# Attention by single key blocks from the third block of an image on, and outputs at fixed places of a block

## The chip, the cores and the metric

The kernel runs on one core of a Trainium2 chip. The metric is the device time of one execution in microseconds. The times shown are of three runs, of which the median counts; a profile was taken of one further execution.

## What is computed

The input x is four images of 128 channels and 64 x 64 points, all in 32-bit floats. Cut to what matters here:

```python
x = x + conv_part(group_norm(x))          # layer 0: convolution, norms, and a selective scan (Mamba)
t = tokens(x)                             # 4 images x 4096 tokens x 128
qkv = layer_norm(t) @ W_qkv + b_qkv       # 4 heads of 32
scores = einsum('bhnd,bhmd->bhnm', q, k) / sqrt(128)
t = t + (softmax(scores) @ v) @ W_proj + b_proj
t = t + experts(layer_norm(t))            # 8 experts, the two best of each token, weighted
```

The scan of layer 0 runs along the 4096 points of an image: h = da * h + du for 16 states of each channel. The attention is over all 4096 tokens of the same image. So an image's attention needs keys and values of all its points, while queries and keys of a point exist as soon as layer 0 is done there.

## The kernel before

**Units of work.** An image is cut into 8 blocks of 512 points. The kernel's main loop (L1207 to L1254, the `while slot < len(units) ...` loop) runs *slots*. Each of the slots 0 to 1023 holds one unit of the scan: image b, block i, channel half p, state n, in this order, so that a block takes 32 slots. A unit is one exponential on ScalarE (da), a multiply, the scan itself and a second multiply on VectorE (tiles h and hc), and a matmul with the identity that sums over the states (y), for single states in the first 128 slots and later for sums of two states, which GpSimd makes.

**Attention groups.** Beside its scan unit a slot holds one attention group, if the generator `attention` has one to give. A group is two key tiles of 128 keys against 1024 queries of one head: four score matmuls (sc), two exponentials of 128 x 1024 (pT), and, one slot later in `weighted`, eight matmuls with the values (av). Each image has 4 query sets (q) x 4 heads x 32 key tiles, so 256 groups, and all four have 1024. The exponential needs no maximum, since the scores' size is bounded ahead, so partial sums over some of the keys may be stored and added later. Groups come in the order of RUNS: one entry is a query set and the key quarters (two blocks each) that it is taken over. In a run each head has its parts (one key quarter, four groups). A run that does not end a query set's keys stores its sum (avs, by way of ScalarE, to the DRAM tile avd); the next run of the same query set loads it as prev and adds it on GpSimd. When the last run of a set is done, the sum goes to the DRAM tile total, `inverted` makes the reciprocals of the softmax's denominators (inverse), and two outputs are put on lane X.

**When a group can run.** `quarters_ready` asks whether the blocks of the part's queries and keys are closed, that is, whether their queries, keys and values are on their way to DRAM. If not, the slot goes on without a group. Groups are taken strictly in order; an image's groups begin when the image before has had its 256. The loads of the next part (ks, v, and qs for a new head) are issued with the second of a part's four groups, on SP's queue, where all loads and stores of the main loop are issued in order. There are 3 buffers of ks and v and 2 of qs, prev and avs, and one PSUM buffer of av.

**Lanes.** Everything else is in two lanes of small steps, X and Y, that advance two steps in each slot (`advance`). Lane Y makes what the scan needs (first_norm, conv, inputs), in a fixed order. Lane X holds `closed` of each block (what comes after the scan, down to keys, queries and values), which is put at its front when the block's scan is done, and the outputs (`finished`: projection, norm, routing, experts, store), which stand at its back. A task of a lane runs to its end before the next begins, so that an output under way delays the next closed. After slot 1023 lane Y takes outputs from lane X as well, if it has nothing else.

**Order.** The wrapper at L445 chains each engine's instructions in the order in which the Python program issues them, so nothing is reordered, and the profile gives L445 for almost every instruction: tiles' names tell them apart. The order, and so the number of slots, is fixed when the program is built. In the program of before there are 1204 slots; the first group is in slot 78, the last in slot 1177.

Of the kernel before, what the change touches and what calls it, by code (L numbers as in the profile page):

```python
# [9 lines left out]
F32 = mybir.dt.float32  # L10
F32R = mybir.dt.float32r
# [6 lines left out]
P = 128  # L18
C = 128
EPS = 1e-5  # L20
BLK = 512
NT = BLK // P
IMG = 64
DI = 64
NST = 16
DH = 32
NH = 4
# [9 lines left out]
def conv_mamba_attn_moe_kernel(ctx: ExitStack, tc: tile.TileContext, t: dict):  # L37
    nc = tc.nc
    x, out = t["x"], t["out"]
    B, _, L = x.shape  # L40
    NB = L // BLK
# [727 lines left out]
    def closed(b, i):  # L769

        if i == 0:
            kqv[b] = [], [], [], dram.tile([P, NTILE * C], F32, name="td")
        kd, qd, vd, td = kqv[b]
        j, u = divmod(i, 2)
        if u == 0:
            kd.append(dram.tile([P, 2, 2 * BLK], F32, name=f"kd{j}"))
            qd.append(dram.tile([P, 2, 2, 2 * BLK], F32, name=f"qd{j}"))
            vd.append(dram.tile([NH, 2, P, NT * 2 * DH], F32, name=f"vd{j}"))
        kd, qd, vd, sj = kd[j], qd[j], vd[j], slice(u * BLK, (u + 1) * BLK)
        s = slice(i * BLK, (i + 1) * BLK)  # L780
        cm = tmp("X", "cm")
        vector.scalar_tensor_tensor(
            cm.rearrange(IMAGE, w=IMG), xn_of[b, i][:, 3:].rearrange(IMAGE, w=IMG), skip,
            y0_rows(b, i), ALU.mult, ALU.add,
        )
        xr = load_x(t["xtok"][b], i, "xr")
        yield
        yield
        ps = work("X")
        for p in range(2):  # L790
            r = slice(DI * p, DI * p + DI)
            mm(ps[r, :], wout[:, p, r], gated.pop((b, i, p)))
        done.add(("freed", b, i))
        yield
        vector.tensor_add(cm, ps, cm)
        gpsimd.tensor_add(by_tile(xr), by_tile(xr), projb[:, None, :].to_broadcast([P, NT, C]))
        yield
        while held:
            yield
            yield  # L800
        held.add("closed")
        ps = transposed("X", by_tile(cm))
        yield
        xt = yield from normalised("X", by_tile(ps))
        held.clear()
        ps = transposed("X", xt)
        yield
        f = tmp("X", "f")
        scalar.activation(f, ps, AF.Identity, bias=lnb, scale=lnw)
        yield  # L810
        ps = work("X", [P, NT, C])
        for j in range(NT):
            mm(ps[:, j, :], f[:, j * P : (j + 1) * P], projT)
        yield
        tt = side.tile([P, NT, C], F32, name="tt")
        vector.tensor_add(tt, ps, by_tile(xr))
        send(tsave[b][:, s], tt.rearrange("p j c -> p (j c)"), 2)
        xt = yield from normalised("X", tt)

        tr = tmp("X", "tr", [P, NT, C])  # L820
        gpsimd.tensor_add(tr, tt, crow[:, None, :].to_broadcast([P, NT, C]))
        send(td[:, s], tr.rearrange("p j c -> p (j c)"), 2)
        ps = transposed("X", xt)
        yield
        xa = tmp("X", "xa")
        scalar.copy(xa, ps)
        yield
        for d, w, bias in ((kd, wkn, bkn), (qd, wqn, bqn)):
            ps = work("X")
            mm(ps, w, xa)  # L830
            yield
            hi = side.tile([P, BLK], F32R, name="hi", bufs=2)
            vector.tensor_scalar(hi, ps, bias, None, ALU.add)
            lo = side.tile([P, BLK], F32R, name="lo", bufs=2)
            vector.scalar_tensor_tensor(
                lo, ps, bias, hi.bitcast(F32), ALU.add, ALU.subtract
            )
            for half, w in enumerate((hi, lo)):
                w = w.bitcast(F32)
                if len(d.shape) == 4:  # L840
                    send(d[:, :, half, sj], w[:, None, :].to_broadcast([P, 2, BLK]))
                else:
                    send(d[:, half, sj], w)
            yield
        ps = work("X", [P, NT, NH, DH])
        for j in range(NT):
            mm(ps[:, j].rearrange("p h d -> p (h d)"), xa[:, j * P : (j + 1) * P], wv)
        yield
        vector.tensor_copy(vst[:, :, :, 0:DH], ps.rearrange("p j h d -> p h j d"))
        send(vd[:, u].rearrange("h p q -> p h q"), vst.rearrange("p h j d -> p h (j d)"))  # L850
        yield
# [2 lines left out]

    STEP, PART = 2, 8

    def queries(b, qp, h):

# [2 lines left out]
        sync.dma_start(out=qs.bitcast(F32), in_=src)  # L863
        return qs

    def keys(b, h, k):

        ks = att.tile([P, PART * P], F32R, name="ks", bufs=3)
        src = kqv[b][0][k][DH * h : DH * h + DH].rearrange("d a l -> (d a) l")
        sync.dma_start(  # L870
            out=ks.bitcast(F32), in_=src[:, None, :].to_broadcast([2 * DH, 2, PART * P])
        )
        return ks

    def values(b, h, k):
        v = att.tile([P, PART // NT, NT, 2 * DH], F32, name="v", bufs=3)
        sync.dma_start(
            out=v.rearrange("p i j d -> p i (j d)"),
            in_=kqv[b][2][k][h].rearrange("i p q -> p i q"),
        )  # L880
        return v

# [1 line left out]


    RUNS = (
        (0, (0, 1)), (1, (0, 1)), (2, (0, 1, 2)), (0, (2,)), (0, (3,)), (1, (2, 3)), (2, (3,)),
        (3, (0, 1, 2, 3)),
    )

    def quarters_ready(b, *quarters):
        return all(("closed", b, 2 * j + 1) in done for j in quarters)

    def attention(b):


        seen, parts = [], []
        for q, ks in RUNS:
            final = sum(len(k) for p, k in seen if p == q) + len(ks) == NB // 2
            for h in range(NH):  # L900
                for k in ks:
                    parts.append((q, h, k, k == ks[0], k == ks[-1], any(p == q for p, _ in seen), final))
            seen.append((q, ks))

        def load(part, qs=None):
            q, h, k, first, _, more, _ = part
            prev = None
            if qs is None:
                qs = queries(b, q, h)
            if first and more:  # L910
                prev = att.tile([P, BLK], F32, name="prev", bufs=2)
                sync.dma_start(out=prev, in_=partial.pop((b, q, h)))
            return qs, keys(b, h, k), values(b, h, k), prev

        ahead = None
        for at, part in enumerate(parts):
            q, h, k, first, last, _, final = part
            if ahead is None:
                while not quarters_ready(b, q, k):
                    yield None  # L920
                ahead = load(part)
                for _ in range(2):
                    yield None
            qs, ks, v, was = ahead
            ahead = None
            if first:
                prev = was
            for g in range(0, PART, STEP):
                if g >= STEP and ahead is None and at + 1 < len(parts):
                    nxt = parts[at + 1]  # L930
                    if quarters_ready(b, nxt[0], nxt[2]):
                        ahead = load(nxt, qs if nxt[:2] == (q, h) and not nxt[3] else None)
                pTs = []
                for j in range(g, g + STEP):
                    sc = ps_sc.tile([P, 2, BLK], F32, name="sc")
                    for u in range(2):
                        mm(
                            sc[:, u, :], ks[:, j * P : (j + 1) * P],
                            qs[:, u * BLK : (u + 1) * BLK],
                        )  # L940
                    pT = att.tile([P, 2, BLK], F32, name="pT", bufs=4)
                    scalar.activation(pT, sc, AF.Exp, scale=ATT_SCALE)
                    pTs.append((v[:, j // NT, j % NT, :], pT))
                yield (
                    b, q, h, pTs, first and g == 0, last and g + STEP == PART, prev, final,
                )

    sums, partial, total, inverse, later = [None], {}, {}, {}, deque()
# [31 lines left out]
    def inverted(b, q):  # L980
# [7 lines left out]
            )  # L988
        yield
        vector.reciprocal(den, den)  # L990
        inverse[b, q] = d = dram.tile([2, NH, BLK], F32, name="inverse")
        send(d.rearrange("u h (a n) -> (u h a) n", n=n), den)
        yield
        for u in range(2):
# [132 lines left out]
    def advance(lane, second):  # L1127
# [3 lines left out]
        while True:  # L1131
            if lane not in running:

                tasks = lanes[lane] if lanes[lane] or slot < len(units) else lanes["X"]
                if not tasks or not all(k in done for k in tasks[0][2]):
                    return False
                key, stages, _ = tasks.popleft()
                running[lane] = key, stages(lane) if callable(stages) else stages
# [229 lines left out]
```

## Time and profile before

| what | value |
|---|---|
| runs shown | 5581.73, 5587.63, 5599.81 us; median 5587.63 |
| profiled execution, its own time | 5602.77 us |
| span of the profile | 5600.4 us |
| mean granted TensorE clock | 0.944 |
| exponentials of the attention (pT) | 2048 of 1022 ns on ScalarE |
| value matmuls (av), score matmuls (sc) | 8192 and 4096, 2004.9 and 1308.8 us busy |
| scan (h), with and without a start value | 1024 in all, 1464 and 1429 ns on VectorE |
| loads of rows, ks, v, qs | 1024, 256, 256, 129 issues; 512, 512, 256, 512 KB |
| DMA | 1097.91 MB, 58.5% of 16 engines' time |

The profile is of one execution on one core. Busy shares are averages over the span; the slices and the stretches asked for one by one tell its stages apart. PE is TensorE's matmuls, PEld its weight loads, DVE VectorE, ACT ScalarE, POOL GpSimd, SP the queue that issues the DMAs. Times of a stretch are counted from the start of the span.

### The profile page before, as it was taken

What the parts mean: (1) busy time and instruction counts of PE and PEld (TensorE: products, weight loads), DVE (VectorE), ACT (ScalarE), POOL (GpSimd) and SP (SyncE); (2) the same over time, 40 slices, a digit from 0 to 9 for tenths busy, and PEclk for the clock granted to TensorE, in tenths of its full rate; (3) what the DMA queues carried; (4) which work ended last, traced back from release to release, by engine and by line L of the source; (5) the groups of instructions that cost most, each with busy time, mean ns of one, the idle gap of its engine ahead of it and who ended that gap; (6) DMA issues with size and microseconds to landing.
All of it is one profiled execution on the core that took longest, in us unless ns stands there. A gap on an engine that the chain in (4) does not pass through costs nothing.

```text
span 5600.4 us, 60586 instructions
## 1 busy us (share of the span) xinstructions
PE 4916.5 (88%) x17866; PEld 2040.8 (36%) x17866; DVE 4174.5 (75%) x6275; ACT 3892.2 (69%) x5957; POOL 2161.8 (39%) x1885
## 2 busy tenths in 40 slices
PE   4666798988999988999998899898999989899997
PEld 2222333333333333333333333333333333344343
DVE  4888877887888888887887888887888888741221
ACT  3455587787777777787777777687777777666553
POOL 2333444454444444445443444444444443320000
PEclk7777799999999999999999999999999999999998
DMA  3455566666666666667665556666765666654432
GB/s 95 169 171 176 194 210 210 205 228 211 230 208 203 210 208 216 205 225 229 224 211 192 192 200 213 219 221 209 232 223 202 206 205 209 210 183 154 147 121 67
DMA packets 427635, 1097.91 MB, mean 196 GB/s; under 512 B 48401, under 2 KB 131746, under 8 KB 427298
## 3 DMA queue, kind: packets, MB, share of 16 engines
q1 hardware_dynamic: 426130, 1093.17, 58.5%
q8 instruction: 144, 2.36, 0.2%
q14 instruction: 193, 1.58, 0.1%
q10 hardware_dynamic: 1168, 0.80, 0.1%
HBM read 941.95 MB, written 135.00 MB: 192 GB/s over the span
## 4 chain that ended last, share of the span: by engine, by line
PE 45%; DVE 21%; ACT 15%; issue 7%; POOL 6%; DMA 5%; SPq 1%; DVEq 0%; ACTq 0%; POOLq 0%
PE av L445 17%; DVE h L445 11%; PE sc L445 10%; PE ps_X L445 8%; PE ps_Y L445 5%; ACT pT L445 5%; PE y L445 4%; ACT L445 3%; ACT xt L445 3%; DVE hc L445 2%; DVE cm L445 2%; POOL rsY L445 1%; POOL rsX L445 1%; DMA ks<-kd 1%; ACT da L445 1%
## 5 line engine op out<-in xcount | busy, mean ns | idle before, releaser
L445 ACT ACTIVATE pT<-sc 128x1024 f32<-128x1024 f32 x2048 | 1983.7, 1022 | 1017.6 <-PE sc L445 1015.2
L445 PE MATMUL av<-pT,v 128*64 128x512 f32 x8192 | 2004.9, 610 | 3.5 <-ACT avs L445 3.3
L445 DVE TENSOR_TENSOR_SCAN h<-da,state,h 128x512 f32<-128x512 f32 x896 | 1311.3, 1464 | 118.6 <-ACT da L445 26.8
L445 PE MATMUL sc<-qs,ks 128*128 128x512 f32 x4096 | 1308.8, 440 | 96.9 <-DMA ks<-kd 51.9
L445 POOL TENSOR_TENSOR hc<-hc 128x512 f32<-128x512 f32 x448 | 655.8, 1465 | 1718.7 <-DVE hc L445 1513.3
L445 PEld LDWEIGHTS sc<-qs,ks 128*128 128x128 f32 x4096 | 717.7, 193 | 773.7 <-ACT pT L445 283.0
L445 PEld LDWEIGHTS av<-pT,v 128*64 128x64 f32 x8192 | 501.6, 137 | 1193.3 <-issue 1105.8
L445 DVE TENSOR_TENSOR h<-rows,du 128x512 f32<-128x512 f32 x1024 | 830.6, 811 | 88.0 <-ACT state L445 38.1
L445 DVE TENSOR_TENSOR hc<-rows,h 128x512 f32<-128x512 f32 x1024 | 802.2, 783 | 78.3 <-DVE h L445 2.3
L445 ACT ACTIVATE da<-delta,amat 128x512 f32<-128x512 f32 x1024 | 749.4, 732 | 9.4 <-DVE h L445 5.2
L445 PE MATMUL y<-hc,ident 128*128 128x512 f32 x1152 | 661.5, 662 | 62.4 <-DVE hc L445 51.3
L445 ACT ACT_TABLE_LOAD x319 | 409.3, 1283 | 22.9 <-PE ps_Y L445 17.8
L445 ACT COPY state<-h 128x1 f32<-128x1 f32 x896 | 175.7, 196 | 194.8 <-DVE h L445 194.3
L445 PEld LDWEIGHTS y<-hc,ident 128*128 128x128 f32 x1152 | 219.6, 209 | 213.8 <-DVE hc L445 101.4
L445 POOL TENSOR_SCALAR rsY<-mvY 128x4 f32<-128x4 f32 x99 | 57.5, 581 | 527.3 <-DVE mvY L445 523.2
L445 POOL TENSOR_TENSOR avs<-avs,prev 128x512 f32<-128x512 f32 x64 | 89.3, 1396 | 438.1 <-ACT avs L445 319.7
L445 PE MATMUL ps_X<-share,w_ew 128*128 128x512 f32 x448 | 223.9, 622 | 20.5 <-DVE share L445 20.2
L445 ACT ACTIVATE xt<-ps_Y,shiftY,rsY 128x128 f32<-128x128 f32 x380 | 143.2, 462 | 129.9 <-POOL shiftY L445 122.4
L445 POOL TENSOR_SCALAR du<-e 128x512 f32<-128x512 f32 x64 | 145.9, 2280 | 217.2 <-ACT e L445 217.2
L445 DVE TENSOR_TENSOR share<-share,xf 128x1024 f32<-128x1024 f32 x128 | 182.8, 1428 | 51.1 <-DMA share<-sharesY 31.0
L445 DVE RECIPROCAL den<-den 128x32 f32<-128x32 f32 x16 | 5.5, 346 | 265.6 <-DMA den<-total 265.6
L445 DVE TENSOR_TENSOR_SCAN h<-da,h 128x512 f32<-128x512 f32 x128 | 182.9, 1429 | 17.3 <-ACT da L445 4.4
(234 smaller groups left out, 4729.6 us busy)
## 6 DMA issues: line engine op xcount, KB each, us to landing
rows<-bcd SPq DMA_DIRECT2D x1024, 512.0 KB
ks<-kd SPq DMA_DIRECT2D x256, 512.0 KB
qs<-qd SPq DMA_DIRECT2D x129, 512.0 KB
v<-vd SPq DMA_DIRECT2D x256, 256.0 KB
share<-sharesX SPq DMA_DIRECT2D x112, 512.0 KB
pairs<-xn SPq DMA_DIRECT2D x128, 128.5 KB
qd<-hi SPq DMA_DIRECT2D x32, 512.0 KB
qd<-lo SPq DMA_DIRECT2D x32, 512.0 KB
```

The lines of the kernel that those rows point to most:

```text
L445: return lambda *args, **kw: queued(op(*args, **kw))
```

## The change

RUNS is now written in single blocks: (query set, first key block, end). There are ten runs per image instead of eight. The first takes query set 0 over key blocks 0 to 2, the second query set 1 over 0 to 3, and so on; a part is still cut at the quarters' borders, so that it has two blocks (four groups) or one (two groups). Of the 20 parts of each head 8 have one block; before there were 16 parts per head, all of two. `ready` asks for all blocks up to the last that the part needs. The loads of the next part are issued from three groups before the part's end on, which in a part of one block is its first group. The sum of before (prev) is loaded with the first group of the last part of a run, not with the run's first part. In `advance` an output may begin only in slots 2 to 17 of each 32, until four slots after the scan's end. Two kinds of DRAM tiles have more buffers: td three, inverse four (two before).

```diff
-    STEP, PART = 2, 8
+    STEP = 2
...
-    def keys(b, h, k):
+    def keys(b, h, k, u, n):
...
+        src = src[:, u * BLK : (u + n) * BLK]
...
     RUNS = (
-        (0, (0, 1)), (1, (0, 1)), (2, (0, 1, 2)), (0, (2,)), (0, (3,)), (1, (2, 3)), (2, (3,)),
-        (3, (0, 1, 2, 3)),
+        (0, 0, 3), (1, 0, 4), (0, 3, 5), (1, 4, 5), (2, 0, 6), (1, 5, 7), (0, 5, 8), (1, 7, 8),
+        (2, 6, 8), (3, 0, 8),
     )
...
+    def ready(b, part):
+        last = max(2 * part[0] + 1, 2 * part[2] + part[3] + part[4] - 1)
+        return all(("closed", b, i) in done for i in range(last + 1))
...
+            cuts = [lo, *range(lo + 2 - lo % 2, hi, 2), hi]
             for h in range(NH):
...
+                for k0, k1 in zip(cuts, cuts[1:]):
+                    parts.append((
+                        q, h, k0 // 2, k0 % 2, k1 - k0, k0 == lo, k1 == hi, known > 0,
+                        seen[q] == NB,
+                    ))
...
-            for g in range(0, PART, STEP):
-                if g >= STEP and ahead is None and at + 1 < len(parts):
+            for g in range(0, NT * n, STEP):
+                if g == 0 and last:
+                    prev = None
+                    if more:
+                        prev = att.tile([P, BLK], F32, name="prev", bufs=2)
+                        sync.dma_start(out=prev, in_=partial.pop((b, q, h)))
+                if g >= NT * n - 3 * STEP and ahead is None and at + 1 < len(parts):
...
-        inverse[b, q] = d = dram.tile([2, NH, BLK], F32, name="inverse")
+        inverse[b, q] = d = dram.tile([2, NH, BLK], F32, name="inverse", bufs=4)
...
                 if not tasks or not all(k in done for k in tasks[0][2]):
+                    return False
+
+                if (
+                    tasks[0][0][0] == "out" and slot < len(units) + 4
+                    and not 2 <= slot % (2 * NST) < NST + 2
+                ):
                     return False
```

Values are cut in the same way as keys, and td has `bufs=3`.

More of the change, by code (lines that the diff above doesn't have):

```diff
@@ L771, in closed @@
         if i == 0:
-            kqv[b] = [], [], [], dram.tile([P, NTILE * C], F32, name="td")
+            kqv[b] = [], [], [], dram.tile([P, NTILE * C], F32, name="td", bufs=3)
         kd, qd, vd, td = kqv[b]
@@ L864, in queries, with values @@
         return qs
-    def keys(b, h, k):
-        ks = att.tile([P, PART * P], F32R, name="ks", bufs=3)
+    def keys(b, h, k, u, n):
+        ks = att.tile([P, 2 * BLK], F32R, name="ks", bufs=3)
         src = kqv[b][0][k][DH * h : DH * h + DH].rearrange("d a l -> (d a) l")
+        src = src[:, u * BLK : (u + n) * BLK]
         sync.dma_start(
-            out=ks.bitcast(F32), in_=src[:, None, :].to_broadcast([2 * DH, 2, PART * P])
-        )
-        return ks
-    def values(b, h, k):
-        v = att.tile([P, PART // NT, NT, 2 * DH], F32, name="v", bufs=3)
+            out=ks[:, : n * BLK].bitcast(F32),
+            in_=src[:, None, :].to_broadcast([2 * DH, 2, n * BLK]),
+        )
+        return ks
+    def values(b, h, k, u, n):
+        v = att.tile([P, 2, NT, 2 * DH], F32, name="v", bufs=3)
         sync.dma_start(
-            out=v.rearrange("p i j d -> p i (j d)"),
-            in_=kqv[b][2][k][h].rearrange("i p q -> p i q"),
+            out=v[:, :n].rearrange("p i j d -> p i (j d)"),
+            in_=kqv[b][2][k][h, u : u + n].rearrange("i p q -> p i q"),
         )
@@ L886, in conv_mamba_attn_moe_kernel @@
     RUNS = (
-        (0, (0, 1)), (1, (0, 1)), (2, (0, 1, 2)), (0, (2,)), (0, (3,)), (1, (2, 3)), (2, (3,)),
-        (3, (0, 1, 2, 3)),
-    )
-    def quarters_ready(b, *quarters):
-        return all(("closed", b, 2 * j + 1) in done for j in quarters)
+        (0, 0, 3), (1, 0, 4), (0, 3, 5), (1, 4, 5), (2, 0, 6), (1, 5, 7), (0, 5, 8), (1, 7, 8),
+        (2, 6, 8), (3, 0, 8),
+    )
+    def ready(b, part):
+        last = max(2 * part[0] + 1, 2 * part[2] + part[3] + part[4] - 1)
+        return all(("closed", b, i) in done for i in range(last + 1))
     def attention(b):
-        seen, parts = [], []
-        for q, ks in RUNS:
-            final = sum(len(k) for p, k in seen if p == q) + len(ks) == NB // 2
-            for h in range(NH):
-                for k in ks:
-                    parts.append((q, h, k, k == ks[0], k == ks[-1], any(p == q for p, _ in seen), final))
-            seen.append((q, ks))
+        seen, parts = {}, []
+        for q, lo, hi in RUNS:
+            known = seen.get(q, 0)
+            seen[q] = known + hi - lo
+            cuts = [lo, *range(lo + 2 - lo % 2, hi, 2), hi]
+            for h in range(NH):
+                for k0, k1 in zip(cuts, cuts[1:]):
[3 more added lines that the diff above has]
+                    ))
+        assert all(n == NB for n in seen.values())
         def load(part, qs=None):
-            q, h, k, first, _, more, _ = part
-            prev = None
+            q, h, k, u, n = part[:5]
             if qs is None:
                 qs = queries(b, q, h)
[L910 to L913, printed above, removed]
+            return qs, keys(b, h, k, u, n), values(b, h, k, u, n)
+        prev = None
         ahead = None
         for at, part in enumerate(parts):
-            q, h, k, first, last, _, final = part
+            q, h, k, _, n, first, last, more, final = part
             if ahead is None:
-                while not quarters_ready(b, q, k):
+                while not ready(b, part):
                     yield None
@@ L923, in attention @@
                     yield None
-            qs, ks, v, was = ahead
+            qs, ks, v = ahead
             ahead = None
-            if first:
-                prev = was
-            for g in range(0, PART, STEP):
-                if g >= STEP and ahead is None and at + 1 < len(parts):
+            for g in range(0, NT * n, STEP):
+                if g == 0 and last:
+                    prev = None
+                    if more:
+                        prev = att.tile([P, BLK], F32, name="prev", bufs=2)
+                        sync.dma_start(out=prev, in_=partial.pop((b, q, h)))
+                if g >= NT * n - 3 * STEP and ahead is None and at + 1 < len(parts):
                     nxt = parts[at + 1]
-                    if quarters_ready(b, nxt[0], nxt[2]):
-                        ahead = load(nxt, qs if nxt[:2] == (q, h) and not nxt[3] else None)
+                    if ready(b, nxt):
+                        ahead = load(nxt, qs if nxt[:2] == (q, h) and not nxt[5] else None)
                 pTs = []
@@ L944, in attention @@
                 yield (
-                    b, q, h, pTs, first and g == 0, last and g + STEP == PART, prev, final,
+                    b, q, h, pTs, first and g == 0, last and g + STEP == NT * n, prev, final,
                 )
```

## Prediction

> **What bounds the kernel now.** I read the page's busy shares and slices first, then stretches of the span one by one, then the chain. The program's main loop runs one *slot* after another: slot 0 to 1023 each hold one scan step and, once attention has begun, one attention group (4 score matmuls, 2 exponentials, 8 value matmuls); after slot 1023 only attention groups and outputs are left.
>
> ```profile
> span 5600.4 us, 60586 instructions
> PE 4916.5 (88%) x17866; PEld 2040.8 (36%) x17866; DVE 4174.5 (75%) x6275; ACT 3892.2 (69%) x5957; POOL 2161.8 (39%) x1885
> ...
> PE   4666798988999988999998899898999989899997
> ...
> DVE  4888877887888888887887888887888888741221
> ...
> PEclk7777799999999999999999999999999999999998
> ```
>
> PE is the busiest engine, but the slices show three stages. In the first four slices or so DVE leads and PE is half empty, with its clock at 0.7; in the middle PE leads with DVE close behind; in the last five DVE falls to 1 or 2 tenths and PE stays at 9. The same in stretches (us, then busy time and count of PE, PEld, DVE, ACT, POOL, the PE clock, the DMA share, GB/s):
>
> ```profile
> 102.00:515.00 413.00, 276.04 (x601) 110.38 (x602) 353.81 (x496) 204.80 (x399) 143.28 (x126) 0.77 0.51 170
> ...
> 1144.00:4965.00 3821.00, 3471.49 (x12979) 1445.71 (x12976) 3162.20 (x4649) 2858.97 (x4402) 1674.67 (x1417) 0.97 0.64 213
> 4965.00:5527.00 562.00, 549.24 (x2218) 228.29 (x2216) 92.86 (x252) 337.03 (x391) 39.58 (x52) 0.99 0.39 127
> 5527.00:5600.40 73.40, 38.51 (x102) 20.03 (x100) 26.87 (x75) 7.72 (x17) 3.42 (x8) 0.64 0.28 92
> ```
>
> The third line is the tail: 562 us in which PE is 98% busy with attention alone. The prices come from narrower stretches, cut at slot borders:
>
> ```profile
> 515.30:584.80 69.50, 40.12 (x72) 13.23 (x70) 62.12 (x81) 34.42 (x66) 20.42 (x17) 0.73 0.52 170
> 782.00:869.50 87.50, 85.67 (x315) 33.64 (x314) 67.01 (x81) 73.36 (x111) 35.81 (x27) 1.00 0.62 210
> ...
> 5131.00:5209.70 78.70, 77.56 (x318) 34.84 (x316) 27.49 (x74) 42.70 (x55) 7.24 (x11) 1.00 0.41 139
> ...
> 5340.70:5412.70 72.00, 71.64 (x294) 32.52 (x292) 25.34 (x72) 37.72 (x50) 3.42 (x8) 1.00 0.37 122
> 5412.70:5526.40 113.70, 113.70 (x460) 43.82 (x460) 0.00 (x0) 74.78 (x78) 0.00 (x0) 1.00 0.21 67
> ```
>
> Line 1 is slots 110 to 129: 20 scan steps without attention, 3.48 us each. Line 2 is slots 174 to 193, the same place two blocks later, with a group in each: 4.38 us. A group put beside a scan step there costs 0.90 us. The last line is 38 groups of the tail with nothing beside them: 2.99 us each, PE busy throughout. Lines 3 and 4 are 17 and 16 tail slots with two outputs beside them. The chain agrees on who sets the end:
>
> ```profile
> PE 45%; DVE 21%; ACT 15%; issue 7%; POOL 6%; DMA 5%; SPq 1%; DVEq 0%; ACTq 0%; POOLq 0%
> ```
>
> **What the Trainium skill says.** "TensorE: Matmul & The Clock Gate", Part 1, says that the array runs at half clock by default and at full clock after about 3.4 us of sustained work. The trace agrees: 0.73 in slots 110 to 129, 1.00 with groups in the same place, so PE's extra work there arrives on a faster clock. "ScalarE: Activation LUTs", on table sets, says that copies are in every set and that a load takes about 1283 ns; the trace's table loads have a mean of 1283 ns, and the only ScalarE instructions that the change adds are copies (avs), so I add no loads. "DMA: Bandwidth & Descriptors", in its anatomy of one DMA, says that completion is counted only when the last byte is confirmed, about 2.0 us beside the bytes; its fit gives 3.2 us for 512 KB, an estimate for another issuing path. Here key loads on the chain took 4.0 to 11.5 us, so the trace decides.
>
> **The change part by part.** Both programs' orders are fixed when they are built, so slots can be counted. Each has 1024 groups. The program of before has 1204 slots, the last group in slot 1177; the changed one has 1183, the last group in 1156. Lane Y is the same, slot by slot.
>
> *Earlier begin.* Before, attention has 4 groups at slot 78, then none until 142. The change adds 20 groups at 110 to 129 (three blocks known), loses 4 at 198 to 201, and fills five empty slots at 465 to 469. So 21 groups leave the tail, 21 x 2.99 = 62.8 us off. They come back at 0.90: 18.9 us on. Bounds: 0 (all in PE's gaps) to 2.99 each; the measured pair of stretches decides.
>
> *One output per block.* The outputs are the same 32. Before, a block of 32 slots has either few or none, or about 1.3 beside the scan; after, one in nearly all. I take levelling at nothing: what an output needs moves from one block to another, and costs alike. But two outputs of image 2 move out of the scan stage into slots 1026 to 1052 of the tail. In the tail a pair costs 78.7 - 17 x 2.99 = 27.9, or 72.0 - 16 x 2.99 = 24.2: 26 us for two. In the scan stage:
>
> ```profile
> 1144.00:1303.00 159.00, 138.96 (x507) 55.48 (x504) 123.30 (x158) 121.41 (x188) 76.48 (x62) 0.96 0.66 220
> ...
> 1467.00:1627.00 160.00, 147.50 (x566) 62.44 (x566) 135.46 (x216) 124.30 (x200) 77.25 (x67) 0.98 0.69 225
> ```
>
> The first block has no output, the second 1.3. With two more blocks of each kind PE's mean is 139.4 and 148.4, so one output is 9.0 / 1.3 = 6.9 us of PE, while time differs by 4.4. I take 6.9: 14 off for two. Net 12 on (bounds 8 to 20).
>
> *The inverse.* In 5254.6 to 5340.7, 16 to 17 slots of outputs took 86.1 us, some 11 more than the like pairs: the vector multiply of aT waited 23.3 us for the load of inv, and PE behind it. After, this pair and the next begin 18 slots after their last group, not 10, so inverse has long been written. The inv load itself still takes its time; I take 6 off (0 to 11).
>
> *Ten runs for eight.* Per image and head two more runs: 32 more each of query loads (512 KB), avs copies (589 ns on ACT), sums with prev (1396 ns on POOL) and stores and loads of avd (256 KB each). ACT is 75% and POOL 44% busy in the middle stage, so they lie beside PE; but PE's next av waits for the copy, since there is one av buffer. In all of before, the value matmuls and their weight loads waited 3.3 + 16.6 us for it over 128 ends; I take 0.15 us each, 5 on (0 to 32 x 1.99 = 64).
>
> *Smaller parts.* Parts go from 256 to 320; 128 of these hold one block and last two groups. The next keys and values are asked for at the first of them, two slots ahead instead of three: some 10 us in the middle stage, 6 in the tail. SP issues in order, so a load also stands behind rows and prev loads and their buffers' releases; PE's queue, with the scan's y and the lanes' matmuls, stands behind a late score. Before, it waited:
>
> ```profile
> PE sc L445 <- DMA ks<-kd: 51.9, 9, 10.6
> ```
>
> Nine waits at three slots' lead (the longest 10.6). At two slots a landing of 8 us or more begins to show, but most of the loads are half as large. I take 0.08 us for each of 128, 10 on. Bounds: 0, and 1 us each, 128.
>
> *Buffers of avs.* Two runs per image now take one block, so that a head lasts two groups (32 heads in all). There are two avs buffers, and in about half of these heads the copy to avs comes one slot or so after the store of the head two before was issued. A late store holds ACT, and PE behind it. I take 2 on (0 to 30).
>
> *The rest* (three td, four inverse buffers in DRAM) frees waits and issues nothing: zero.
>
> Sum: -62.8 + 18.9 + 12 - 6 + 5 + 10 + 2 = -20.9, call it 21. The profiled execution took 5602.8 (its span and 2.4 us around): 5582 by its own time. It stood 15 above the median of the runs shown; I take the difference off the median: 5587.6 - 21 = 5567.
>
> **The rivals.**
> (1) *Late keys take the gain.* The one on the other side. Without the load term the sum is -31. The measurement can tell about 0.3%, 17 us, from no change; so it is slower by more than that when 128 s > 48, s = 0.37 us per one-block part, in the scan stage above all, where SP waits for rows buffers. At 0.6 us: 5587.6 - 31 + 77 = 5633 or so. For it: key loads of 11 us on the chain; against it: nine waits in all, and half-size loads.
> (2) *Given back in small coin.* Outputs in the tail at their upper price (+8), run ends at 0.4 us (+8), loads at 0.15 (+9): 5567 + 25 = 5592, no change that can be told.
> (3) *More than counted.* Groups at 110 to 129 fit PE's gaps (40 of 69.5 us busy) at 0.4 us (-10), and levelling pays since blocks with a crowded lane X have more waits by PE (-15): 5567 - 25 = 5542.
> That it does not start earlier is excluded by the program's order.
>
> **How the numbers follow.** Forecast (5550 to 5571): 0.45. Rival 3, below 5550: 0.17. Rival 2, 5571 to 5604: 0.26. Rival 1, above: 0.12. Faster by over 0.3% is 0.62, within 0.26, slower 0.12. The range 5535 to 5602 leaves about 0.07 below and 0.13 above; the likeliest case's own is 5550 to 5571.
>
> **What would show it.** The time from the last scan step to the end falls from 636 to about 590 us; slots 110 to 129 take about 87 us at a clock near 1.0; plain tail groups stay at 2.99; tail slots with the two moved outputs cost some 26 more than plain ones; the score's wait for keys stays below 70 us. I am wrong if the stretch from slot 288 to 1023 grows by over 20 us, with that wait above 100, or if the tail's plain groups leave 2.99.

## The result, and the profile after

The changed kernel takes 5560.12 us (median of four runs, 5556.45 to 5562.85) against 5589.66 of before (the three runs shown and one more, 5581.73 to 5599.81): a ratio of 0.9946, with a 95% interval of 0.9928 to 0.9963, so faster by 0.4 to 0.7%. The profiled execution has a span of 5561.1 us. The profiled execution of before lay 13 us above its kernel's median, that of after 3 us above; a comparison of the two traces (spans 39.3 us apart) therefore shows some 10 us more gain than the medians do.

The page of the profile after: span, busy time, the slices of PE, DVE and the granted clock, and the chain by engine.

```profile
span 5561.1 us, 61179 instructions
PE 4907.1 (88%) x17866; PEld 2045.2 (37%) x17866; DVE 4182.2 (75%) x6275; ACT 3897.4 (70%) x5989; POOL 2208.9 (40%) x1917
...
PE   4667798999899899999999999999899899999997
...
DVE  4888778888887888888888888887888788862221
...
PEclk7778899999999999999999999999999999999998
...
PE 46%; DVE 18%; ACT 13%; DMA 7%; POOL 7%; issue 7%; SPq 1%; DVEq 0%; ACTq 0%; POOLq 0%
```

PE has the same matmuls. The clock rises a slice or two earlier, and VectorE's last slices begin later in the span: the tail is shorter. In stretches cut at the same slots as those that the prediction used (us, busy time and count of each engine, clock, DMA share, GB/s): up to slot 110, slots 110 to 255, slots 256 to the last scan step, the tail's groups, and the end.

```profile
102.80:515.80 413.00, 274.92 (x596) 110.64 (x596) 352.86 (x495) 204.68 (x399) 143.49 (x126) 0.77 0.51 170
515.80:1173.50 657.70, 579.99 (x2054) 235.12 (x2056) 517.36 (x687) 492.25 (x750) 292.84 (x241) 0.95 0.64 212
1173.50:4969.20 3795.70, 3463.71 (x12942) 1443.26 (x12938) 3142.98 (x4573) 2867.33 (x4422) 1705.07 (x1433) 0.97 0.66 220
4969.20:5487.50 518.30, 508.19 (x2063) 216.93 (x2064) 119.05 (x326) 300.92 (x364) 43.91 (x60) 1.00 0.42 141
5487.50:5561.10 73.60, 38.08 (x106) 20.01 (x102) 26.61 (x75) 7.71 (x17) 3.41 (x8) 0.66 0.28 91
```

The same stretches of before, in the same order:

```profile
102.20:515.30 413.10, 276.34 (x602) 110.38 (x602) 353.91 (x496) 204.60 (x399) 143.28 (x126) 0.77 0.51 171
515.30:1144.10 628.80, 539.03 (x1858) 217.26 (x1858) 515.35 (x686) 459.38 (x710) 280.81 (x233) 0.92 0.60 203
1144.10:4964.80 3820.70, 3471.19 (x12979) 1445.55 (x12976) 3161.97 (x4648) 2858.87 (x4402) 1674.57 (x1417) 0.97 0.64 213
4964.80:5526.40 561.60, 548.84 (x2217) 228.39 (x2217) 93.06 (x252) 337.03 (x391) 39.58 (x52) 0.99 0.39 128
5526.40:5600.40 74.00, 39.11 (x106) 20.10 (x102) 26.87 (x75) 7.72 (x17) 3.42 (x8) 0.64 0.28 91
```

The gain is in the tail: 43.3 us off its groups, 0.4 off the end. The scan stage gets 28.9 us longer where attention now begins, and 25.0 shorter in the rest: 4 longer together by the two profiles. If the tail took as long in the other executions, it is some 14 longer by the medians (29.5 in all against 43.7 in the tail). Five narrower stretches of after: slots 110 to 129, a pair of outputs in the tail (16 slots) and plain groups (29) of the tail, which answer to those of before; then slots 1026 to 1052, which hold the two outputs that moved, and the next pair of outputs (17 slots).

```profile
515.80:607.70 91.90, 85.63 (x296) 34.85 (x296) 61.73 (x81) 70.03 (x105) 19.74 (x17) 0.96 0.63 207
...
5325.80:5397.80 72.00, 71.63 (x294) 32.52 (x292) 25.35 (x72) 37.70 (x50) 3.41 (x8) 1.00 0.35 121
5397.80:5484.60 86.80, 86.80 (x350) 33.57 (x348) 0.00 (x0) 56.80 (x60) 0.00 (x0) 1.00 0.21 66
4982.60:5095.70 113.10, 110.37 (x462) 49.26 (x460) 34.29 (x97) 65.68 (x87) 16.58 (x23) 1.00 0.48 165
5172.00:5253.80 81.80, 76.54 (x305) 33.82 (x304) 28.87 (x77) 41.25 (x54) 9.79 (x13) 0.98 0.56 190
```

The first was 69.5 us without groups: 22.4 more for 20 groups, 1.12 each, at a clock of 0.96 instead of 0.73. The plain groups give 86.8 / 29 = 2.99 us, as before.

### The profile page after: what moved, and what is told of

It reads as the page before. It is cut to its first block, busy times and chain, and to the rows that moved or that the text cites. A ratio compares the mean times of both kernels' runs of the same rounds, so it can differ in the third digit from the quotient of the medians.

```text
span 5561.1 us, 61179 instructions
## 1 busy us (share of the span) xinstructions
PE 4907.1 (88%) x17866; PEld 2045.2 (37%) x17866; DVE 4182.2 (75%) x6275; ACT 3897.4 (70%) x5989; POOL 2208.9 (40%) x1917
## 4 chain that ended last, share of the span: by engine, by line
PE 46%; DVE 18%; ACT 13%; DMA 7%; POOL 7%; issue 7%; SPq 1%; DVEq 0%; ACTq 0%; POOLq 0%
PE av L445 17%; PE sc L445 10%; DVE h L445 9%; PE ps_X L445 8%; PE ps_Y L445 6%; PE y L445 5%; ACT pT L445 4%; ACT xt L445 3%; ACT L445 2%; DMA rows<-bcd 2%; POOL rsY L445 2%; DMA ks<-kd 2%; DVE hc L445 2%; POOL rsX L445 1%; DVE cm L445 1%
## 5 line engine op out<-in xcount | busy, mean ns | idle before, releaser
L445 DVE TENSOR_TENSOR_SCAN h<-da,state,h 128x512 f32<-128x512 f32 x896 | 1339.2, 1495 | 106.7 <-ACT da L445 12.5
L445 POOL TENSOR_TENSOR hc<-hc 128x512 f32<-128x512 f32 x448 | 641.6, 1434 | 1829.3 <-DVE hc L445 1669.9
L445 DVE TENSOR_TENSOR hc<-rows,h 128x512 f32<-128x512 f32 x1024 | 807.7, 789 | 79.4 <-DVE h L445 2.3
L445 POOL TENSOR_TENSOR avs<-avs,prev 128x512 f32<-128x512 f32 x96 | 145.8, 1518 | 341.8 <-ACT avs L445 258.7
L445 ACT COPY avs<-av 128x512 f32<-128x512 f32 x160 | 94.1, 588 | 162.4 <-PE av L445 133.8
```

Source lines behind the costliest of these rows:

```text
L445: return lambda *args, **kw: queued(op(*args, **kw))
```

## The experiments

Theory: slots that leave the tail are worth 2.99 us each and cost about 1 in the scan stage; the rest are small prices. Rivals: late keys or small parts eat the gain; levelling the outputs over the blocks is what pays; run ends cost more than thought. A run end is what each head needs where a run stops: the copy of its sum out of PSUM and a store, and, when the query set goes on, a load of that sum (prev), an addition and a new load of queries. The changed kernel was not run again in these groups of runs, so a distance "from the changed kernel" is the difference of the two ratios to before, times 5590 us. Runs of one kernel lie up to 30 us apart, and single blocks of the scan stage differ by some us between executions, so distances below 10 us are not told apart. The changed kernel's own ratio is known to 0.0018, which puts 10 us of doubt on every such distance; but two kernels that should hardly differ from it (less lead for the keys, parts of one block) came out within 2 us of it.

**The rule for outputs alone.** The kernel before, with this and the buffer counts:

```diff
+                if (
+                    tasks[0][0][0] == "out" and slot < len(units) + 4
+                    and not 2 <= slot % (2 * NST) < NST + 2
+                ):
+                    return False
```

> The kernel before with the rule for outputs (and the two buffer counts) alone, runs of quarters as before. 1199 slots instead of 1204, last group in slot 1172; one output (the last of image 2) moves into the tail. If a slot saved is worth 2.99 us in the tail and costs about 1 in the scan stage, and an output moved costs some 6 net: 5 x 2 - 6 = 4 us faster than before, not to be told from it. If levelling the outputs over the blocks is what pays, 15 to 25 us faster, and nearly all of the change's gain is here.

Measured: 5581.81 (ratio 0.9986, interval 0.9978 to 0.9994), 7 to 8 us faster. With the old runs, levelling is not what pays: the scan stage's outputs are as level here as in the changed kernel, and three quarters of the gain are missing.

**The runs alone.** The changed kernel without the five lines above.

> The changed kernel without the rule for outputs. 1192 slots, last group in slot 1165; all outputs of images 0 to 2 stay in the scan stage, and slots 465 to 473 have no group. If slots saved set the time: 12 x (2.99 - 1.0) = 24 us faster than before, less what run ends and late keys cost (5 to 15). If levelling is what pays: no gain, or slower by the cost of more runs and parts.

Measured: 5607.73 (1.0033, 1.0020 to 1.0046): 19 us slower than before, with 12 slots fewer. Its tail took 594.3 us, 41 less than before; the scan stage took all of it back and more (in the profiles 43 longer than before, against 4 in the changed kernel). So new runs seem to carry costs that the prediction's sum had too low, and they pay only together with the rule, which gives 9 slots more (without it a block closes late and slots 465 to 473 stand empty) and takes two outputs out of the scan stage. By the prices found below these two are worth some 25 of the 48 us between this kernel and the changed one; where the rest comes from, levelling with the new runs included, is not shown.

**No early groups.**

```diff
-                while not ready(b, part):
+                while not ready(b, part) or 82 <= slot < 142:
```

> The changed kernel, but no group in slots 82 to 143, so that attention goes on where the kernel before does. 1196 slots instead of 1183; everything else is the same, the runs, parts and outputs too. If a slot moved from the tail to the scan stage is worth 2.99 - 1.1: 13 x 1.9 = 25 us slower than the changed kernel, so some 5585. If early groups fit PE's gaps: 13 x 2.6 = 34 slower. If the gain came from elsewhere (outputs, parts): within 8 us of the changed kernel.

Measured: 5596.07 (1.0012, 1.0004 to 1.0020), 37 us from the changed kernel: 13 slots at 2.8 us. The tail grew by 37.6, so almost nothing came back in the scan stage although slots 110 to 129 took 69.4 us again. Without the early begin the rest of the change is not faster than before. How much of the 37 us is the groups' new place against the blocks, and not the slots, this run cannot tell; the shifts below come back to it.

**Lane Y takes outputs from slot 1000 on.**

```diff
-                tasks = lanes[lane] if lanes[lane] or slot < len(units) else lanes["X"]
+                tasks = lanes[lane] if lanes[lane] or slot < len(units) - 24 else lanes["X"]
...
-                    tasks[0][0][0] == "out" and slot < len(units) + 4
+                    tasks[0][0][0] == "out" and slot < len(units) - 24
```

> The changed kernel, but from slot 1000 on the rule for outputs ends and lane Y, which is nearly empty there, takes outputs too. 1183 slots as before; the last three outputs of image 2 begin at slots 1000, 1004 and 1016, so that the two that the change moved into the tail run mostly in the scan stage. If an output costs 12 in the tail and 7 beside the scan, about 10 us faster than the changed kernel, some 5550. If the scan stage has no room for two lanes of outputs (VectorE leads there), no faster, or slower.

Measured: 5565.63 (0.9961, 0.9948 to 0.9975), 8 us above the changed kernel, so no gain. In the profile the last block grew by 19.6 us for 1.4 outputs more, and the tail shrank by 15.1. Taking outputs out of the tail saves nothing, because an output costs at least as much beside the scan. That turned the question round, and led to late outputs below.

**More run ends.**

```diff
-        (0, 0, 3), (1, 0, 4), (0, 3, 5), (1, 4, 5), (2, 0, 6), (1, 5, 7), (0, 5, 8), (1, 7, 8),
-        (2, 6, 8), (3, 0, 8),
+        (0, 0, 3), (1, 0, 4), (0, 3, 5), (1, 4, 5), (2, 0, 2), (2, 2, 6), (1, 5, 7), (0, 5, 8),
+        (1, 7, 8), (2, 6, 8), (3, 0, 4), (3, 4, 8),
```

> The changed kernel with two of its runs cut in two between quarters (query set 2 over blocks 0 to 2 and 2 to 6, query set 3 over 0 to 4 and 4 to 8): 32 more run ends, each with a query load, a copy of avs, a store, a load of prev and a sum; parts, slots (1183) and outputs stay. By the prediction's price of 0.15 us an end: 5 us slower than the changed kernel, not to be told. By what the first four experiments' block times suggest (some 1 us an end in the scan stage): 32 slower or a little less, as 4 of them lie in the tail. If the copy and the sum were wholly exposed: 64.

Measured: 5585.90 (0.9991, 0.9983 to 0.9999): 25 us from the changed kernel, 0.8 us for each of 32 ends (0.5 to 1.1 with the two intervals).

**Less lead for the keys.**

```diff
-                if g >= NT * n - 3 * STEP and ahead is None and at + 1 < len(parts):
+                if g >= NT * n - 2 * STEP and ahead is None and at + 1 < len(parts):
```

> The changed kernel, but every part of two blocks asks for the next keys and values two slots ahead instead of three, as the parts of one block do. 192 parts lose a slot of lead. If late keys cost what the rival of the prediction needs (0.37 us a part): 70 us slower than the changed kernel. By the prediction's 0.08: 15 slower. By the unchanged wait for keys in the profile after: within 8 us of it.

Measured: 5560.91 (0.9949, 0.9937 to 0.9961): 2 us from the changed kernel. The rival's price for late keys (70 us here) is excluded, and the prediction's 15 are not seen. PE's wait for them (us in total, times, longest), first after, then with the shorter lead:

```profile
PE sc L445 <- DMA ks<-kd: 51.9, 15, 7.5
```

```profile
PE sc L445 <- DMA ks<-kd: 61.8, 23, 7.0
```

**Outputs of image 2 late.**

```diff
-                    and not 2 <= slot % (2 * NST) < NST + 2
+                    and not (slot < 836 and 2 <= slot % (2 * NST) < NST + 2)
```

> The changed kernel, but no output begins between slots 836 and 1027: all eight outputs of image 2 run in the tail, in both lanes, staggered by half an output, 1183 slots as before. Six more outputs leave the scan stage. If an output costs 14 us there, as the block times suggest, and 12 in the tail: 6 x 2 = 12 us faster than the changed kernel. By the prediction's 6.9 in the scan stage: 6 x 5 = 30 us slower.

Measured: 5531.44 (5527.08 to 5534.31; 0.9892, 0.9878 to 0.9906): 30 us faster than the changed kernel, and the fastest here. The same three blocks (slots 832 to 863, 864 to 895, 928 to 959), first after, with an output in each, then with late outputs, with none:

```profile
4035.00:4193.90 158.90, 145.00 (x548) 61.16 (x548) 131.01 (x195) 119.76 (x189) 69.93 (x61) 0.98 0.61 204
4193.90:4350.10 156.20, 144.56 (x550) 60.78 (x549) 130.93 (x195) 120.12 (x189) 67.65 (x59) 0.99 0.62 204
4510.50:4669.90 159.40, 147.03 (x549) 61.84 (x549) 128.79 (x195) 120.91 (x191) 67.15 (x60) 0.97 0.63 206
```

```profile
4032.40:4174.90 142.50, 130.92 (x493) 51.89 (x492) 119.64 (x159) 115.42 (x179) 68.51 (x57) 0.99 0.62 205
4174.90:4317.50 142.60, 133.79 (x501) 52.67 (x499) 118.11 (x157) 117.42 (x183) 66.02 (x55) 0.99 0.61 201
4462.50:4607.60 145.10, 135.71 (x503) 52.97 (x499) 116.76 (x157) 118.46 (x184) 64.77 (x55) 0.98 0.61 201
```

Here an output is 16.4, 13.6 and 14.3 us of time, with 14.1, 10.8 and 11.3 us of PE and about 12 of DVE. Over all six blocks the scan stage took 92 us less, 15.3 for an output; the tail, 654.9 us now, took 63.0 more (591.9 in the changed kernel), 10.5 for each.

**Attention 13 and 6 slots later.**

```diff
-        group = next(groups, None)
+        group = None if 207 <= slot < 220 else next(groups, None)
```

and the same with 213 in place of 220.

> The changed kernel with its 20 early groups, but without groups in slots 207 to 219, so that all later groups stand 13 slots later, exactly where they stand without the early groups. 1196 slots. If the place of runs and parts against the blocks' lanes makes no difference: the tail's 13 x 2.99 = 39 less some 12 in the emptied slots, 27 us slower than the changed kernel, slots 288 to 1023 as in it. If that place matters, as the scan stage without the early groups suggests (25 us more in slots 288 to 1023 for the same work): 50 us slower.

> The changed kernel without groups in slots 207 to 212 alone, so that later groups stand 6 slots later; 1189 slots. If the place of attention against the blocks made no difference, the 13-slot shift would have cost 39 less about 4, and this one costs 18 less about 2, some 16 us over the changed kernel. The 13-slot shift cost 49. If the place matters and the changed kernel's is a lucky one, 25 to 35 over it; if it matters from slot to slot without order, anything from 5 to 35.

Measured: 5608.83 (1.0035, 1.0022 to 1.0047) for 13 slots, 50 us from the changed kernel; 5573.12 (0.9965, 0.9953 to 0.9978) for 6 slots, 11 us from it. Six slots cost less than their 18 us in the tail, as a slot's price in the scan stage would have it; thirteen cost 11 more than their 39. At 2.99 - 1.12 a slot, 24 and 11 were due. So the place of the groups against the blocks has an influence of up to some 25 us that does not follow the number of slots. Which work collides there is not settled.

**Parts of one block in the last run.**

```diff
-            cuts = [lo, *range(lo + 2 - lo % 2, hi, 2), hi]
+            cuts = list(range(lo, hi + 1)) if q == 3 else [lo, *range(lo + 2 - lo % 2, hi, 2), hi]
```

> The changed kernel with the last query set's run (a fifth of the groups in two block parts) cut into parts of one block: 64 more parts, 128 more of one block in place of 64 of two; bytes, runs, sums, outputs and slots (1183) stay. If small parts cost by themselves (late keys, more issues): 0.37 us for each of 128 is 47 us slower than the changed kernel. If run ends are what cost and parts are free: within 8 us of it.

Measured: 5560.36 (0.9943, 0.9930 to 0.9956): the changed kernel's time. The 47 us of the rival are excluded, and no cost of small parts is seen, though one of some 10 us could not be told; an end of a run costs more.

**Late outputs with the old runs.** The first experiment with the rule of late outputs.

> The kernel before with its own runs, the rule for outputs, and no output between slots 836 and 1027 (the same as in the changed kernel with late outputs): 1199 slots, six outputs fewer in the scan stage than with the rule alone. If an output costs 15 beside the scan and 10.5 in the tail whatever the runs are: 6 x 4.8 = 29 us faster than with the rule alone, some 5553, and the changed kernel's runs are then worth 16 slots and some 22 us, as 5531 is below it. If late outputs pay only with the new runs: no faster than 5575.

Measured: 5579.63 (5561.54 to 5583.58; 0.9970, 0.9958 to 0.9982), 9 us faster than the rule alone, not 29. In its profile slots 800 to 1023 took 93 us less than with the rule alone, as expected, but the tail took 76 more, 12.7 for an output, and the slots before 800 some 14 more. The two programs are the same up to slot 836, so these 14 are a difference between executions; without them the two traces give 16 us of gain. The price beside the scan (15) held; that in the tail, and so the net gain, depends on the kernel.

**Queries loaded for each part.**

```diff
-                        ahead = load(nxt, qs if nxt[:2] == (q, h) and not nxt[5] else None)
+                        ahead = load(nxt)
```

> The changed kernel, but the queries of a head are loaded anew for each of its parts: 159 more loads of 512 KB, nothing else added; slots 1183, runs and outputs stay. More runs cost some 0.8 us an end, and an end brings a query load, a load of prev, a store of avs, a copy and a sum. If the loads are what costs, 0.5 us or more each: 80 us or more over the changed kernel. If it is the copy on ScalarE, the sum on GpSimd and the wait for them: within 10 us of it.

Measured: 5573.96 (0.9966, 0.9955 to 0.9978): 11 us from the changed kernel, 0.07 for each of 159 loads of 512 KB. With the intervals it is at most 0.15, so the query load is the smaller part of an end's 0.8 us. What of the rest is the copy, the sum, the store or the load of prev was not taken apart. One wait grew with the ends, though that it is what costs the time is not shown: that of ScalarE for the last value matmul ahead of its copy, behind which the next exponentials stand; before, after, and with 32 more ends:

```profile
ACT avs L445 <- PE av L445: 75.3, 73, 5.7
```

```profile
ACT avs L445 <- PE av L445: 133.8, 93, 5.7
```

```profile
ACT avs L445 <- PE av L445: 160.3, 112, 5.6
```

## Why the prediction was right, and which terms were not

Forecast: 21 us off, 5567 us. Measured: 29.5 off, 5560.1. The main mechanism was right, and so was the place of the gain: the time from the last scan step to the end fell from 635.6 to 591.9 us (about 590 forecast), slots 110 to 129 took 91.9 (about 87), and plain tail groups stayed at 2.99. Several prices were not right, and their errors cancel for the most part; that the sum came out so near is in part luck.

- **Earlier begin** (-62.8, back +18.9): right. 21 slots fewer, 2.99 us for a plain tail group; in place a group cost 1.12, not 0.90, which makes 23.5 for 21. The two stretches behind the 0.90 differed in more than the groups: up to slot 127 y is summed for single states, so slots 110 to 129 hold 38 y matmuls (20.4 us in the trace of after), slots 174 to 193 only 22 (11.3 us in that of before). The Trainium skill ("TensorE: Matmul & The Clock Gate", Part 1) says that the array's clock is halved unless matmuls keep it busy; the trace agrees, with a mean clock of 0.73 without groups and 0.96 with them. What a slot is worth in the whole kernel scatters: 2.8 us in the kernel without early groups, 1.8 and 3.8 in the two shifts.
- **Two outputs into the tail** (+12): wrong in size, and by the price below in sign. In the tail they cost about what was forecast. The pair in 5131.0 to 5209.7 stood beside 18 slots, not 17 (its 318 PE matmuls are 24 more than those of the pair with 16 slots, and a group has 12), so that the pairs of before cost 78.7 - 18 x 2.99 = 24.9 and 24.2 us, not 26. After, slots 1026 to 1052 took 113.1 us, 27 x 2.99 = 80.7 of it for the groups and 9.4 for the last closed (42.3 for 11 slots in the trace of before, less 32.9), so 23.0. The term that fails is "one output is 9.0 / 1.3 = 6.9 us of PE". With the runs kept, an output is 15.3 us beside the scan, so the two moved outputs gain 30.6 - 23.0 = 7.6. The blocks compared in the prediction differed in their runs as well, and those without outputs held more ends (8, 7 and 6 copies of avs against 5, 5 and 6), but at 0.8 us an end that is only some 1.3 us a block. What else made them dear is open.
- **The inverse** (-6): right in size. The three pairs of outputs before the last took 31.0, 24.2 and 24.2 us beyond their plain groups, together 79.4 against 84.4 before (24.9, 35.3 and 24.2): 5 off. One long wait stayed and now falls on the first pair (81.8 us for 17 slots), which still begins 10 slots after its last group, as all three did before. Two of those three, at 24.9 and 24.2 us, show no such wait, so the ten slots alone do not explain it.
- **Ten runs for eight** (+5): the mis-sized term on the other side. 0.15 us an end was taken from the wait of the value matmuls alone. 32 more ends cost 25 us when they were added by themselves, 0.8 each, so some 25 here.
- **Smaller parts** (+10): none seen. Less lead for 192 parts and 64 parts more each left the time within 2 us, where about 10 can be told. PE's wait for keys is 51.9 us before and after.
- **Buffers of avs** (+2): not seen apart from the ends.

With these prices the sum is -62.8 + 23.5 - 7.6 - 5 + 25 + 0 = -26.9, against -29.5. By stages, the tail comes to -62.8 + 23.0 - 5 = -44.8, where the traces show -43.7, and the scan stage to 23.5 - 30.6 + 25 = 17.9, where they show 4 and the medians some 14. That agreement should not be taken for more than it is. With the same prices the runs alone come out near the time of before (12 slots at 2.99 - 1.12 gain 22, 28 to 32 ends cost as much), and measured 19 slower; the kernel without early groups and the longer shift are 10 to 25 above their sums too. The experiments on ends and outputs each change the place of other work as well, and that alone was worth up to 25 us in the shifts. A second estimate limits this: a least-squares fit to the block times of all fourteen traces (slots 256 to 991, counting ends, outputs and groups in each block, with one constant for each block's number) gives 0.7 to 1.2 us for an end and 11 to 15 for an output beside the scan, depending on which kernels are left out. So ends and outputs both cost more than forecast, but the gain of the two moved outputs may be anything from nothing to 7.6 us, and that the prices simply add is not shown.

Of the rivals, late keys at the price that the rival needs are refuted by two experiments. "Given back in small coin" names what happened to the run ends, and "more than counted" what happened to the outputs, for another reason than the one given: not that levelling pays (with the old runs it does not, as the rule alone shows) but that an output costs less in the tail than beside the scan, clearly so in the kernel with late outputs.

## What to carry to other kernels

When work moves between a stage where one engine is the bound and one where two are close to it, price it from a pair of stretches that differ in this work alone; here stretches that differed in other work too gave about half of an output's price or less. Look then at what fills the tail: the change shortened it by moving attention forward, but the tail, where VectorE was a quarter busy and ScalarE about half, was also the cheaper place for outputs, and sending six more there gave as much again as the change did. With the old runs the same step gave only 9 us, so such a price has to be measured in the kernel at hand. A regrouping that starts work earlier has to be charged for each end of a group, not for the loads alone.

## What was not expected of the hardware

Loads were far cheaper than the chain's pieces of 4 to 11 us suggest: 159 more query loads of 512 KB (83 MB, on some 1130) cost 11 us, give or take 12, at a mean DMA busy share of about 0.6. And one more run end, whose copy from PSUM takes 0.59 us on an engine that is 70% busy and whose sum takes 1.5 us on one that is 40% busy, cost about 0.8 us on the whole, though PE is the busiest engine.
